# Four graph layers on one core: stages in another order, pieces of two PSUM banks, and a planner that keeps to a matmul form

## The chip, the core and the metric

One Trainium2 chip, one of its cores. The engines are TensorE (PE: matmuls and, beside them, its weight loads, PEld), VectorE (DVE), ScalarE (ACT), GpSimd (POOL) and SyncE (SP, which here only issues DMAs). The metric is device time of one execution in microseconds (us), the median of five runs.

## The reference, cut to what matters

x is 16 batches of 1024 nodes by 256 features; adj is one 1024 by 1024 adjacency matrix for all. Four layers follow each other, each of the form x = x + layer(relu(layernorm(x))):

```python
# layers 0, 1 (one head) and 3 (four heads): graph attention
h = x @ W;  e = leaky_relu((h @ a1)[:, None] + (h @ a2)[None, :])
x = x + act(softmax(where(adj, e, -big)) @ h)        # act: relu in layer 0, elu in 1 and 3
# layer 2: eight heads of 32
t = softmax(where(adj > 0, q @ k.T / sqrt(32), -big)) @ v
y = layernorm(h + t);  y = layernorm(y + relu(y @ w1 + b1) @ w2 + b2)
x = x + y
```

## The kernel before

A *stage* is one layer of one batch; there are 64. Work of a stage on TensorE:

- **Way in** (`way_in`, lines 700 to 760): for each of 8 tiles of 128 nodes, VectorE takes mean and variance (lines 663, 664), GpSimd the root (667, 668), ScalarE or VectorE normalises, TensorE transposes (`transpose_rows`, line 687, pieces of two tiles, copied out by ScalarE in line 690), and TensorE projects (`project`, line 697; pieces of one tile for graph attention, of half a batch for q and k).
- **Layers 0 and 1**, one head (`gat_item`): VectorE makes the unnormalised weights p (line 926), and TensorE multiplies them with the values (line 944, tile av, full 128 by 128 matmuls of 257 columns).
- **Layer 2**, the dot stage (`dot_item`): for a group of four heads and a tile of 128 nodes, TensorE makes scores of four heads in four row tiles of 32 rows (line 1147, tile sc), ScalarE takes the exp (1160), VectorE masks (1166), and TensorE sums values and totals into column tiles of 32 columns (lines 1178 and 1183). Then come a division (`dot_out`) and `feed_forward` with `finish`: two layernorms, w1 and w2.
- **Layer 3**, four heads in pairs (`pair_item`): weights on VectorE (line 1000), values (1032) and totals (1056) in column tiles of 32.

The source scores of graph attention are needed along a row by every partition. `sources` transposes them (line 873, tile tpr), VectorE copies them (877), SyncE writes them to DRAM (885 or 888) and reads them back spread over 128 partitions (899 or 904, tile r).

**The order is a planner's.** Every piece of work is an `op` with its engine, a cost, the ops it comes after, the buffers it takes and ends, and for TensorE a form: none (full), 132 (row tiles), 32 (column tiles). `forward` places ops one by one: on each engine it looks at the ops that can begin first, within SLACK, and takes the one of the lowest rank; a change of form is charged with SWITCH. `backward` turns the result into due times, which are the ranks of the next play. The best of PLAYS = 8 plays is what is emitted, so the planner's order is each engine's order on the chip.

Buffers are rings, of which a place is taken over from its last holder: p has 9 places of 1024 elements, y 2, hT 4, big 4. PSUM, eight banks, is split by use: sc two places of two banks (scores, and layer 3's totals), acc two of one bank, mm two of one bank (transposes and projections).

The stages were laid in this order:

```python
order = [(0, 0), (0, 1), (1, 0), (1, 1)]
for b in range(0, B, 2):
    order += [(2, b), (2, b + 1), (3, b), (0, b + 2), (3, b + 1), (0, b + 3), (1, b + 2), (1, b + 3)]
```

At the start, the first x, the adjacency (line 384) and layer 0's weights are loaded, VectorE turns the adjacency into flags (line 1372, twice, for != 0 and for > 0), TensorE transposes these (1378) and ScalarE copies them to the two masks (1382).

Of the kernel before, what the change touches and what calls it, by code (L numbers as in the profile page):

```python
# [285 lines left out]
def fast_path(tc, bad, x, adj, l0_w, l0_a, l1_w, l1_a, w_qkv, ln1_g, ln1_b, ln2_g, ln2_b, w1, b1, w2, b2, l3_w, l3_a, out):  # L286
# [3 lines left out]
    assert B % 2 == 0 and B > 2  # L290
# [9 lines left out]
    with ctx:  # L300
# [5 lines left out]
        ps_sc = ctx.enter_context(tc.tile_pool(name="ps_sc", bufs=2, space=PSUM))  # L306
        ps_acc = ctx.enter_context(tc.tile_pool(name="ps_acc", bufs=2, space=PSUM))
        ps_mm = ctx.enter_context(tc.tile_pool(name="ps_mm", bufs=2, space=PSUM))
# [38 lines left out]
        def gat_weights(group, w_heads, a, alpha, name):  # L347
# [10 lines left out]
            ab = work.tile([P, 2 * C], F32, tag="p", name="ab", bufs=9)  # L358
# [17 lines left out]
            return wx, [lambda h=h: fill(h) for h in range(heads)]  # L376

# [24 lines left out]
        b2_row = work.tile([P, 2 * C], F32, tag="p", name="b2_row", bufs=9)  # L402
# [12 lines left out]
        flags = state.tile([P, NT * C], F32, tag="y", name="flags").bitcast(BF16)  # L415
# [17 lines left out]
        SWITCH = {None: 0.15, 132: 0.2, 32: 0.12}  # L433
# [4 lines left out]
        SLACK = 0.2  # L438
# [5 lines left out]
        class Ring:  # L444
# [3 lines left out]
            def __init__(self, bufs, ordered=False):  # L448
                self.bufs, self.ordered, self.laid, self.first = bufs, ordered, 0, []

        class Hold:


            def __init__(self, ring, make, taken=False):
                self.ring, self.make, self.enders, self.taker, self.t = ring, make, [], None, None
                self.number, ring.laid = ring.laid, ring.laid + 1
                if taken:
                    ring.first.append(self)
                    self.t = make()
# [15 lines left out]
        def choose(open_ops, time, begin, key, slack):  # L475

            best = None
            for eng in range(5):
# [5 lines left out]
                if could:  # L484
                    last = min(c[0] for c in could) + slack
                    at, o = min((c for c in could if c[0] <= last), key=lambda c: key[c[1].number])
                    if best is None or at < best[0]:
                        best = (at, o)
# [4 lines left out]
        def forward(rank):  # L493
# [4 lines left out]
            taken = {ring: list(ring.first) for ring in R.values()}  # L498
# [6 lines left out]

            def begin(o):
# [3 lines left out]
                for i, h in enumerate(o.takes):  # L510
                    ring = h.ring
                    k = len(taken[ring]) + sum(g.ring is ring for g in o.takes[:i])
                    if ring.ordered and h.number != k:
                        return None
                    if k >= ring.bufs:
                        old = taken[ring][k - ring.bufs]
# [5 lines left out]
            for _ in ops:  # L522
                at, o = choose(open_ops, time, begin, rank, SLACK)
# [8 lines left out]
                for h in o.takes:  # L532
                    taken[h.ring].append(h)
                    left[h], free[h] = len(h.enders), 0.0
# [10 lines left out]
        def backward(total, played, taken):  # L545

            before = [list(o.after) for o in ops]
            for ring, holds in taken.items():
                for old, h in zip(holds, holds[ring.bufs :]):
                    before[h.taker.number] += [o for o in old.enders if o is not h.taker]  # L550
# [9 lines left out]
            for _ in ops:  # L560
                at, o = choose(open_ops, time, lambda o: ready[o.number], key, 0.0)
# [9 lines left out]
        def play():  # L571
            rank, best = [o.rank for o in ops], None
            for _ in range(PLAYS):
# [3 lines left out]
                rank = backward(*result)  # L577
            for _, _, o in best[1]:
                for h in o.takes:
                    h.t = h.make()  # L580
# [4 lines left out]
            "sc": Ring(2, True), "acc": Ring(2, True), "p": Ring(9, True), "r": Ring(2, True), "y": Ring(2, True),  # L585
            "big": Ring(4, True), "v0": Ring(1, True), "v1": Ring(1, True), "v2": Ring(1, True), "e": Ring(4),
            "mm": Ring(2), "xn": Ring(2), "hT": Ring(4), "stats": Ring(8), "rstd": Ring(8), "inv": Ring(4),
# [7 lines left out]
        def mm(name, shape=(P, HALF), dtype=F32):  # L595
            return psum(ps_mm, "mm", list(shape), name, dtype)

        def buffer(pool, tag, shape, name, dtype=F32):
            bufs = R[tag].bufs
            return Hold(R[tag], lambda: pool.tile(list(shape), dtype, tag=tag, name=name, bufs=bufs))  # L600

# [4 lines left out]
        class Stage:  # L606
# [9 lines left out]
            def buffers(self):  # L616
                L = self.layer

                pair, odd = divmod(self.b, 2)
                if pair == 0:  # L620
                    place = ((2, 1), (0, 2), (1, 0), (2, 1))[L][odd]
                else:
                    place = (3 - ((2, 2), (0, 1), (2, 0), (1, 2))[L][odd] - pair) % 3
                self.vh = buffer(state, f"v{place}", (P, NT * H2 * (D2 + 1)), "v")
                if L == 2:
                    self.qh = buffer(state, "big", (P, KC, N), "qT")
                    self.kh = buffer(state, "big", (P, KC, N), "kT")
# [5 lines left out]
                if L == 3:  # L633
                    self.rh = [buffer(state, "big", (P, 2, N), "r2") for _ in range(self.heads // 2)]
                if L in (2, 3):
                    self.yh = buffer(state, "y", (P, NT, C), "y")
# [19 lines left out]
        def stats_of(src, rank, after, shift=False):  # L656
# [15 lines left out]
            m_op = op(DVE, 0.54, rank, stats, after, takes=[mh, rh])  # L672
# [7 lines left out]
        def transpose_rows(srcs, rank, after, dst, t, func, scale=1.0, ends=()):  # L680

            tph = mm("tp", (P, KC, 2 * P))
# [6 lines left out]
            def copy():  # L689
                nc.scalar.activation(dst.t[:, :, t * P : (t + 2) * P], tph.t, func, scale=scale)  # L690

            a = op(PE, 0.44, rank, turn, after, takes=[tph], ends=ends)
            return op(ACT, 0.48, rank + 0.7, copy, [a], ends=[tph])
# [6 lines left out]
        def way_in(s, t, rank, after):  # L700
            L = s.layer
            n, i = t // TH, t % TH
            if t == 0:
                s.hTh, s.in_ops = {}, {}
                s.norms, s.turns, s.vals, s.vops, s.roots = {}, {}, {}, {}, {}
                s.lead, s.srcs = {}, {}
            if i == 0:
                s.hTh[n] = buffer(state, "hT", (P, KC, HALF), "hT")
            hT = s.hTh[n]
            xt = lambda: xs[s.b][:, t, :]  # L710
            m_op, r_op, mh, rh = stats_of(xt, rank, after, shift=L == 2)
# [3 lines left out]
            if L == 2:  # L715
# [5 lines left out]
                    [r_op] + before, takes=takes + ([s.yh] if t == 0 else []), ends=[mh, rh],  # L721
                )
            else:
                if t % 2 == 0:
                    s.xnh = buffer(work, "xn", (P, 2, C), "xn")
# [783 lines left out]
```

## Time and profile before

| | us |
|---|---|
| five runs, median (lowest to highest) | 4429.75 (4429.71 to 4431.37) |
| the profiled execution | 4429.66 |
| its span, first to last instruction | 4427.9 |
| TensorE busy | 4361.4 |
| VectorE busy | 3378.2 |
| ScalarE busy | 2075.2 |
| GpSimd busy | 1343.9 |

The profile is one execution. A page gives busy times, the chain of work that ended last, and groups of instructions. A timeline merges equal instructions that follow each other on an engine: start, length, engine, line, tiles, shapes, count, and in brackets how long the engine was idle before and who released it. A table of windows gives each engine's busy time in a stretch. Matmuls are pipelined and their ends are modelled, so a start is a better mark than an end. Each 32-bit matmul is two records, a transpose one. The granted TensorE clock was 0.996 on average.

### The profile page before, as it was taken

To read this page: it belongs to the slowest core of one execution; us is meant where nothing else is said; L and a number is where in the kernel's file an instruction comes from. 1 tells how busy PE (TensorE), PEld (TensorE's weight loads), DVE (VectorE), ACT (ScalarE), POOL (GpSimd) and SP (SyncE) were. 2 spreads that over 40 slices of the span, in tenths; PEclk is the share of its full clock that TensorE was granted. 3 is DMA by queue.
4 is the path that set the end of the run, shared out by engine and by line. 5 is a ranking of instruction groups with operands and counts; after the bars stand their busy time and mean duration, and the time that the engine had idled before them with its cause. 6 is when DMAs were issued, how large, how long until landed. Compare 5 with 4: busy or idle time off the path is not lost.

```text
span 4427.9 us, 71264 instructions
## 1 busy us (share of the span) xinstructions
PE 4361.4 (98%) x28090; PEld 2171.4 (49%) x28090; DVE 3378.2 (76%) x5835; ACT 2075.2 (47%) x3345; POOL 1343.9 (30%) x2025
## 2 busy tenths in 40 slices
PE   8999999999999999999999999999999999999998
PEld 6733467334673346633566335653356533565333
DVE  7568885788856887579875798757987579875898
ACT  4456334563345633456335563356533565335552
POOL 3223333233331333214332233312342123421341
PEclk9999999999999999999999999999999999999999
DMA  3000000000000001000110001000011000100001
GB/s 114 6 1 20 25 30 24 1 20 25 29 25 1 20 25 46 8 1 20 38 36 6 1 20 44 30 6 1 20 44 34 1 1 20 44 25 1 1 20 40
DMA packets 59910, 96.66 MB, mean 22 GB/s; under 512 B 6320, under 2 KB 41520, under 8 KB 59568
## 3 DMA queue, kind: packets, MB, share of 16 engines
q1 hardware_dynamic: 59152, 91.51, 6.1%
q8 instruction: 223, 3.65, 0.3%
q14 instruction: 119, 0.97, 0.1%
q10 hardware_dynamic: 416, 0.52, 0.0%
HBM read 74.84 MB, written 17.17 MB: 21 GB/s over the span
## 4 chain that ended last, share of the span: by engine, by line
PE 89%; DVE 7%; POOL 2%; issue 1%; ACT 1%; DMA 0%; DVEq 0%; SPq 0%; POOLq 0%; ACTq 0%
PE pm L697 21%; PE av L944 19%; PE sc L1147 11%; PE acc L1178 10%; PE sums L1183 9%; PE acc L1032 9%; PE sums L1056 4%; PE tp L687 3%; DVE pe L1166 2%; DVE p L1000 1%; POOL y L1242 1%; POOL rstd L668 1%; DVE y L678 1%; PE tpv L1098 1%; DVE st L663 1%
## 5 line engine op out<-in xcount | busy, mean ns | idle before, releaser
L1166 DVE TENSOR_TENSOR pe<-pe,mask_pos 128x1024 f32<-128x1024 f32 x1024 | 1223.5, 1234 | 343.5 <-ACT pe L1160 342.0
L1160 ACT ACTIVATE pe<-sc 128x1024 f32<-128x1024 f32 x1024 | 998.0, 1022 | 637.0 <-PE sc L1147 594.7
L944 PE MATMUL av<-v,p 128*128 128x257 f32 x4096 | 945.3, 380 | 0.2 <-DVE p L926 0.2
L944 PEld LDWEIGHTS av<-v,p 128*128 128x128 f32 x4096 | 763.4, 190 | 147.4 <-issue 40.9
L667 POOL TENSOR_SCALAR rstd<-stats 128x1 f32<-128x1 f32 x768 | 368.0, 479 | 1262.0 <-DVE stats L664 1238.4
L1000 DVE SCALAR_TENSOR_TENSOR p<-r,e,mask_pos 128x1024 f32<-128x1024 f32 x512 | 635.3, 1281 | 33.6 <-PE sums L1056 33.5
L1147 PE MATMUL sc<-qT,kT 32*128 32x512 f32 x4096 | 590.6, 640 | 0.0
L668 POOL TENSOR_TENSOR rstd<-rstd,minus_half 128x1 f32<-128x1 f32 x768 | 566.8, 738 | 64.0
L1178 PE MATMUL acc<-pe,v 128*32 128x512 f32 x4096 | 549.7, 604 | 0.0
L1183 PE MATMUL sums<-pe,pick 128*32 128x512 f32 x4096 | 538.4, 592 | 0.9 <-ACT o L966 0.9
L1032 PE MATMUL acc<-p,v 128*32 128x512 f32 x4096 | 465.2, 594 | 0.0
L697 PE MATMUL pm<-l_wx,hT 128*128 128x259 f32 (+1 forms) x1536 | 410.8, 398 | 6.0 <-ACT hT L690 2.9
L1242 POOL TENSOR_TENSOR y<-y,turned 128x512 f32<-128x512 f32 x64 | 106.2, 1680 | 1020.4 <-DVE turned L1235 1020.4
L697 PEld LDWEIGHTS pm<-l_wx,hT 128*128 128x128 f32 x1536 | 276.4, 190 | 193.9 <-issue 90.3
L1147 PEld LDWEIGHTS sc<-qT,kT 32*128 32x128 f32 x4096 | 166.6, 182 | 318.3 <-issue 150.3
L690 ACT ACTIVATE hT<-tp 128x512 f32<-128x512 f32 x320 | 190.6, 597 | 238.9 <-PE tp L687 238.5
L663 DVE BATCH_NORM_STATS2 st<-x 128x6 f32<-128x256 f32 x512 | 214.8, 420 | 95.2 <-POOL x L970 77.7
L1183 PEld LDWEIGHTS sums<-pe,pick 128*32 128x32 f32 x4096 | 135.7, 110 | 306.0 <-issue 298.5
L1032 PEld LDWEIGHTS acc<-p,v 128*32 128x32 f32 x4096 | 123.3, 110 | 275.5 <-issue 261.1
L697 PE MATMUL pm<-hT,qkv_sb 128*128 128x512 f32 x512 | 246.6, 606 | 0.0
L1056 PE MATMUL sums<-p,e 128*32 128x512 f32 x2048 | 246.4, 597 | 0.0
L970 POOL TENSOR_TENSOR x<-x,o 128x256 f32<-128x256 f32 x128 | 106.6, 833 | 423.5 <-ACT o L966 338.1
(101 smaller groups left out, 4099.5 us busy)
## 6 DMA issues: line engine op xcount, KB each, us to landing
r<-kept SPq DMA_DIRECT2D x64, 512.0 KB
x<-in_x_dram SPq DMA_DIRECT2D x32, 512.0 KB
r<-kept SPq DMA_DIRECT2D x64, 256.0 KB
out_dram<-x SPq DMA_DIRECT2D x64, 256.0 KB
edges<-in_adj_dram SPq DMA_DIRECT2D x8, 512.0 KB
kept<-rows_sb SPq DMA_DIRECT2D x128, 2.0 KB
qkv_sb<-in_L_gnn_w_qkv_dram SPq DMA_DIRECT2D x1, 768.0 KB
kept<-rows_sb SPq DMA_DIRECT2D x32, 4.0 KB
```

The source lines that it names most:

```text
L667: nc.gpsimd.tensor_scalar(rh.t, mh.t[:, 1:2], EPS, None, ALU.add)
L668: nc.gpsimd.tensor_tensor(rh.t, rh.t, minus_half, ALU.pow)
L697: nc.tensor.matmul(dst, lhsT=lhsT[:, k, :], rhs=rhs[:, k, :], start=(k == 0), stop=(k == KC - 1))
L944: nc.tensor.matmul(avh.t[:, : s.hs + 1], lhsT=phs[j // 2].t[:, j % 2, i * P : (i + 1) * P], rhs=s.v[:, j, h, :], start=(j == 0), stop=(j = ...
L1000: nc.vector.scalar_tensor_tensor(ph.t, s.rh[hp].t[:, hh, :], s.e[:, j, col : col + 1], mask_pos[:, j, :], ALU.max, ALU.mult)
L1032: nc.tensor.matmul(acc[n].t[(2 * hh + part) * W : (2 * hh + part + 1) * W, :], lhsT=s.v[:, jj, h, part * W : (part + 1) * W], rhs=p, start ...
L1056: both(lambda jj, n, hh, h, p: nc.tensor.matmul(sums.t[(2 * n + hh) * W : (2 * n + hh + 1) * W, 0, :], lhsT=s.e[:, jj, 2 * H + h : 2 * H + ...
L1147: nc.tensor.matmul(scs[pair].t[:, hh, :], lhsT=s.kh.t[r0 : r0 + D2, g, j * P : (j + 1) * P], rhs=s.qh.t[r0 : r0 + D2, g, cols], start=True ...
L1160: lambda pair=pair: nc.scalar.activation(phs[pair].t, scs[pair].t, AF.Exp, scale=SCALE2),
L1166: lambda pair=pair: nc.vector.tensor_tensor(phs[pair].t, phs[pair].t, mask(), ALU.mult), [ex], tiles=True,
L1178: nc.tensor.matmul(head(acc, i), lhsT=s.v[:, j, g * QUAD + i, :D2], rhs=p(i), start=(j == 0), stop=(j == NT - 1))
L1183: nc.tensor.matmul(head(sums, i), lhsT=pick[:, g, :], rhs=p(i), start=(g == 0 and j == 0), stop=(g == KC - 1 and j == NT - 1),)
```

## The change

- **Order of stages.** A dot stage is now followed by a stage of layer 1, then layer 3, then layer 0, so that one-head stages stand between the column-tiled ones:

```diff
-        for b in range(0, B, 2):
-            order += [(2, b), (2, b + 1), (3, b), (0, b + 2), (3, b + 1), (0, b + 3), (1, b + 2), (1, b + 3)]
+        order = [(0, 0), (0, 1), (1, 0), (1, 1), (2, 0), (0, 2), (3, 0)]
+        for b in range(1, B - 3):
+            order += [(2, b), (1, b + 1), (3, b), (0, b + 2)]
+        E = B - 1
+        order += [(2, E - 2), (1, E - 1), (0, E), (2, E - 1), (1, E), (3, E - 2), (2, E), (3, E - 1), (3, E)]
```

- **PSUM.** ps_sc and ps_mm go. Three places of two banks, u0 to u2, serve scores, totals, transposes and projections. A ring can now be a set, in which any free place is taken (also for y and hT):

```diff
-        ps_sc = ctx.enter_context(tc.tile_pool(name="ps_sc", bufs=2, space=PSUM))
-        ps_mm = ctx.enter_context(tc.tile_pool(name="ps_mm", bufs=2, space=PSUM))
+        ps_u = ctx.enter_context(tc.tile_pool(name="ps_u", bufs=1, space=PSUM))
...
-            "sc": Ring(2, True), "acc": Ring(2, True), "p": Ring(9, True), "r": Ring(2, True), "y": Ring(2, True),
+            "u": Ring(3, is_set=True), "acc": Ring(2, True), "p": Ring(4, True), "r": Ring(2, True), "y": Ring(2, is_set=True),
...
+        def banks(name):
+            return Hold(R["u"], lambda i: ps_u.tile([P, 2, HALF], F32, tag=f"u{i}", name=name))
```

- **Pieces of two banks.** Transposes of four tiles, not two; values of layer 2 for four tiles; q, k and the first feed-forward product for both blocks of 128 features; the second product for four tiles; graph-attention values for two tiles. Each is copied out by ScalarE in one instruction of 1024 elements where it was two of 512 (but not the feed-forward's relu). The p buffers become 4 places of 2048 elements.

```diff
-                for m in range(2 * KC):
-                    queries_keys(s, m, n, rank + 4.0 + 2.2 * m)
+                    two_values(s, n, rank + 2.3, turned)
+                    for m in range(2):
+                        queries_keys(s, m, n, rank + 4.0 + 4.2 * m)
...
-            scs = [psum(ps_sc, "sc", [P, 2, HALF], "sc") for _ in pairs]
-            phs = [buffer(work, "p", (P, 2, HALF), "pe") for _ in pairs]
+            scs = [banks("sc") for _ in pairs]
+            ph = buffer(work, "p", (P, QUAD, HALF), "pe")
```

- **The planner.** An op of another form than TensorE's last counts as due 4 us later than it is; the charges for a change of form and the slack are set anew:

```diff
-        SWITCH = {None: 0.15, 132: 0.2, 32: 0.12}
-        SLACK = 0.2
+        SWITCH = {None: 0.2, 132: 0.21, 32: 0.125}
+        SLACK = 0.1
+        STAY = 4.0
...
-                at, o = choose(open_ops, time, begin, rank, SLACK)
+                at, o = choose(open_ops, time, begin, lambda o: rank[o.number] + STAY * (o.eng == PE and o.form != form), SLACK)
```

- **Prologue.** For the first stage the row of source scores isn't sent through DRAM: TensorE multiplies the scores, broadcast to 128 columns, with the identity, and ScalarE copies the result. The small inputs and the flags use the two y buffers before these are needed:

```diff
+            if s is stages[0]:
+                s.rops = [spread_sources(s, n, rank, lead[n * TH : (n + 1) * TH]) for n in range(NH)]
+                return
...
+        def spread_sources(s, n, rank, lead):
+            pmh, held = psum(ps_acc, "acc", [P, HALF], "spread"), s.rh[n]
+            def product():
+                for i in range(TH):
+                    nc.tensor.matmul(
+                        pmh.t[:, i * P : (i + 1) * P], lhsT=s.e[:, n * TH + i, 0:1].to_broadcast([P, P]), rhs=ident,
+                        start=True, stop=True,
+                    )
+            a = op(PE, 1.0, rank, product, lead, takes=[pmh], ends=[s.eh])
+            return op(ACT, 0.48, rank + 1.0, lambda: nc.scalar.copy(held.t, pmh.t), [a], takes=[held], ends=[pmh])
```

## The prediction

> **What bounds the kernel now.** I read the page first, then TensorE's timeline, the table of windows, and the ends of the run.
>
> ```profile
> PE 4361.4 (98%) x28090; PEld 2171.4 (49%) x28090; DVE 3378.2 (76%) x5835; ACT 2075.2 (47%) x3345; POOL 1343.9 (30%) x2025
> ...
> PE 89%; DVE 7%; POOL 2%; issue 1%; ACT 1%; DMA 0%; DVEq 0%; SPq 0%; POOLq 0%; ACTq 0%
> ```
>
> TensorE is busy for 98% of the span and is 89% of the chain that ended last. VectorE, at 76%, is second. So the time moves by what TensorE spends, or waits, and by little else. How TensorE spends it is seen in 14 us of its timeline (start, length, line, tile, matmuls):
>
> ```profile
> 1475.22 1.14 PE L1147 MATMUL sc<-qT,kT 32*128 32x512 f32 x8
> 1476.29 1.07 PE L1178 MATMUL acc<-pe,v 128*32 128x512 f32 x8
> 1477.17 1.04 PE L1183 MATMUL sums<-pe,pick 128*32 128x512 f32 x8
> 1478.03 1.04 PE L1178 MATMUL acc<-pe,v 128*32 128x512 f32 x8
> 1478.89 1.04 PE L1183 MATMUL sums<-pe,pick 128*32 128x512 f32 x8
> 1479.86 1.14 PE L1147 MATMUL sc<-qT,kT 32*128 32x512 f32 x8
> 1480.93 1.06 PE L1178 MATMUL acc<-pe,v 128*32 128x512 f32 x8
> 1481.81 1.04 PE L1183 MATMUL sums<-pe,pick 128*32 128x512 f32 x8
> 1482.78 1.99 PE L697 MATMUL pm<-w_sb,hT 128*128 128x256 f32 x8
> 1484.71 1.14 PE L1147 MATMUL sc<-qT,kT 32*128 32x512 f32 x8
> 1485.78 0.66 PE L687 MATMUL tp<-ident,xn 128*128 128x128 f32 x4
> 1486.37 1.06 PE L1178 MATMUL acc<-pe,v 128*32 128x512 f32 x8
> ```
>
> The lengths are modelled, so the distance from start to start is the cost. There are three forms: full (128 rows by 128 columns), row-tiled (32 by 128, the scores) and column-tiled (128 by 32). Column-tiled followed by column-tiled costs 0.86 (1477.17 to 1478.03), followed by another form 0.97 (1478.89 to 1479.86): **leaving it costs 0.11**. Scores cost 1.07 before either form, so leaving them costs nothing that is seen. Eight full matmuls of 256 columns cost 1.93 (1482.78 to 1484.71). Sixteen of 257 cost 3.68:
>
> ```profile
> 1302.39 3.74 PE L944 MATMUL av<-v,p 128*128 128x257 f32 x16
> 1306.07 1.14 PE L1147 MATMUL sc<-qT,kT 32*128 32x512 f32 x8
> ```
>
> The difference of 1.75 for eight gives 0.219 each, so 1.93 holds 0.18 that doesn't grow with the work. The same from 512 columns (four 1.92, eight 3.63) gives 0.21, and from transposes (four 0.59, eight 1.02) 0.16. **A visit to the full form costs about 0.195 with matmuls first, 0.16 with transposes first.**
>
> **The change, part by part.** *Form changes.* In the two programs' instruction order I counted unbroken stretches of one form. Stretches of the full form fall from 680 to 256 (matmuls first 398 to 135, transposes first 282 to 121), because projections now come in two-bank pieces, one-head stages stand between dot stages instead of pairs of dot stages side by side, and the planner keeps to a form. Column-tiled stretches fall from 677 to 547. The matmuls are the same but for eight of 128 columns. Saved: 263 x 0.195 = 51.3, 161 x 0.16 = 25.8, 130 x 0.11 = 14.3, together 91.4. The lowest readings (0.18, 0.16, 0.10) give 86, the highest (0.21, 0.18, 0.114) 99. I take **-93 us**.
>
> The Trainium skill (TensorEngine Tiling (Array Packing), Key Properties) says that changing the tiling mode, not just the tile, drains TensorE, which would price every change alike. All stretches together fall from 1869 to 1299, and 570 x 0.11 would be 63, for 4340. The trace disagrees in that leaving the scores costs nothing, and a visit to the full form more.
>
> *Prologue.* Before, layer 0's first weights wait for VectorE to make all 16 mask flags:
>
> ```profile
> 35.84 5.39 DVE L926 SCALAR_TENSOR_TENSOR p<-r,e,mask_nz 128x512 f32<-128x512 f32 x8
> ...
> 37.16 0.65 PE L944 MATMUL av<-v,p 128*128 128x257 f32 x2
> ```
>
> In the new order eight of the flags (1.14 us apart) come behind these weights, and the row is spread by TensorE and copied by ScalarE, not sent through DRAM (26.30 to beyond 29.39 before). The adjacency has landed by 18 us, so the data allow it. VectorE's work from 9.5 us to the first weights is 14 us: six fills 2.1, three stats 1.8, eight flags 9.1, six small ones 1.3. The first weights then begin near 23.5 and the first av, four weights later, near 27, 10 us earlier. But VectorE remains the fullest engine over the first 60 us of TensorE's work, so part is paid back. I take **-8** (-11 to -3). If the flags still came first it would be 0.
>
> *Stalls.* For each of TensorE's records I took the distance to the next over the lower quartile for the same pair of neighbours. Those over 0.1 us sum to 92 us between 45 and 4412: 40 in the first 1090 us, 17 in the last 550, and 6 to 8 in each 545 us between. The windows agree:
>
> ```profile
> 590.00:1140.00 550.00, 541.16 (x3474) 269.97 (x3466) 416.91 (x710) 255.82 (x413) 171.97 (x249) 0.99 0.06 20
> 1140.00:1685.00 545.00, 542.47 (x3498) 268.85 (x3494) 417.18 (x714) 257.55 (x416) 168.99 (x252) 1.00 0.06 20
> ...
> 4300.00:4428.00 128.00, 110.49 (x895) 40.75 (x891) 111.70 (x164) 24.67 (x45) 18.76 (x30) 0.94 0.11 35
> ```
>
> The first count is TensorE, the third VectorE. Nothing moves off VectorE. I cut both programs into slices of 60 us of undisturbed TensorE work and gave each VectorE instruction its row's mean (these overlap: they sum to 3656 where 3378 are busy). The fullest slice of the middle asks for 1.13 of TensorE's time before and 1.08 after, 1.04 and 1.00 after the overlap: dot (heavy) now alternates with one-head (light). What gets tighter is layer 3's row. Its way before, in the last stage, where nothing else hides it:
>
> ```profile
> 4352.40 0.28 PE L873 MATMUL tpr<-ident,e 128*96 128x128 f32 x1 [0.53 <-DVE v L825]
> ...
> 4354.27 2.95 SPq L888 DMA_DIRECT2D kept<-rows_sb  x8
> 4358.26 1.76 SPq L904 DMA_DIRECT2D r<-kept  x4
> ...
> 4370.71 3.64 PE L1032 MATMUL acc<-p,v 128*32 128x512 f32 x32
> ```
>
> Undisturbed it is: transpose and copy 0.8 (tpr at 2055.8, SP at 2056.57), stores 2.65, 1.1 until the loads issue, 4 until the first half lands (packets until 4362 to 4363), four weights 4.9: 13.5 to 14. The new order puts 11.4 us of TensorE work between this transpose and layer 3's first matmuls; before, it was 41 or more except in the last stage. Behind those stand layer 3's sums, so TensorE waits: 2.5 us in each of 13 repeats, 33. Stalls at the start and the transitional last batches I put at 15, the tail at 25 (17 before), since the last 100 us now ask VectorE for 1.10 of TensorE's time where before it was 1.02. Together 73 for 92: **-19**. From nearly all gone (25) to 157 (8 a repeat, the late chain below) the term is -67 to +65.
>
> *At nothing:* larger evacuations. ScalarE's 512-wide copies (0.597) become 256 of 1024 (1.02 by the exp's row), cheaper per element, at 47% busy; queued dot or av pieces cover the longer hold. The coarser p buffers (4 of 2048 in place of 9 of 1024) are paid in the stalls' range.
>
> A rule speaks against this. The Trainium skill (Perfetto Trace Analysis, Optimizing Scalar/DVE Operations) says that where ScalarE or VectorE isn't saturated but causes bubbles elsewhere, breaking instructions up may let work be completed sooner; the change joins them. If TensorE waited the added 0.42 for each of the 256, it would be 108 and the time 4418.
>
> **Sum.** The profiled execution took 4429.66 (span 4427.9 and 1.8 around it), against the median of 4429.75, so no correction. 4429.7 - 93 - 8 - 19 = **4310**.
>
> **Rivals.** *The forecast*, 4285 to 4345: 60%.
>
> *The row and its chain come late.* In the last stage before, it is 70.5 us from the last dot sums (4300.2) to layer 3's first matmul; the new order has 65 us of TensorE work there. If that pace holds everywhere, 5.5 us more are lost in each of 13 repeats: +72, 4382 (4345 to 4420). For it: the pieces are coarser, so four tiles wait for the slowest. Against: that chain shared VectorE with a full layer-3 stage. 17%.
>
> *Stalls nearly vanish*, as light stages cover the feed-forward chain that costs most now (tp waiting for y): 73 falls to 25, 4262 (4250 to 4285). 16%.
>
> *Slower, by the shared places.* Scores own four banks now; then they, projections and transposes share three places of two. Waits for places exist already where no full-form piece stands between:
>
> ```profile
> 1458.41 1.37 PE L1147 MATMUL sc<-qT,kT 32*128 32x512 f32 x8
> ```
>
> Its 1.37 against 1.14 is 0.23 of waiting for the second exp. Were that paid by all 512 score pieces, it would be 118 and the time 4428; above 0.25 each the change loses, and at 0.4 it gives 4515. Against: with a third place free the next scores need only the first exp, which ends 1 us before they are due, and the third is held only around some 8 projections and transposes per dot stage. 5%, with 2% more for ending within 0.2%.
>
> *Forms not kept* is excluded by the counted order.
>
> Faster by over 0.2% (about 9 us, what a measurement here can tell from no change) is 0.93, the same 0.02, slower 0.05. The range runs from the third case's 4262 to 4380, through the second's own value nearly; what it leaves out is half of the third case, nearly half of the second, and the last.
>
> **What would show it.** After: 1.07 per score piece and about 0.88 and 0.97 for column pieces, unchanged; about 256 stretches of the full form; the first av near 27 us; TensorE's busy time down by about 90; a gap of 2 to 3 us before layer 3's first matmul in each 262-us repeat, released by VectorE's weights. Wrong if score pieces stretch to 1.37 throughout, if the gap per repeat is 8 us or more, or if VectorE ends the chain for long stretches.

## The result and the profile after

| | before | after |
|---|---|---|
| median (lowest to highest), us | 4429.71 (4428.44 to 4431.7) | 4420.42 (4419.07 to 4422.61) |
| runs | 44 | 24 |
| span of the profiled execution | 4427.9 | 4418.7 |
| granted clock, mean | 0.996 | 0.988 |

The ratio is 0.9979 (95% interval 0.9974 to 0.9985): 9.3 us faster, where 120 were forecast. The page of the changed kernel, engines and chain of waits:

```profile
PE 4316.0 (98%) x28105; PEld 2230.8 (50%) x28105; DVE 3377.7 (76%) x5834; ACT 2002.8 (45%) x3091; POOL 1274.2 (29%) x2025
...
PE 92%; DVE 5%; ACT 2%; POOL 1%; issue 1%; DMA 0%; DVEq 0%; SPq 0%; ACTq 0%; POOLq 0%
```

TensorE's busy time fell by 45 us, not by the 90 forecast, and it still ends nearly everything. The lines don't tell whether its work shrank less than thought or whether waits took the place of work. Two views do. The table of windows (TensorE, its weight loads, VectorE, ScalarE, GpSimd, then the granted clock):

```profile
590.00:1140.00 550.00, 540.08 (x3517) 281.00 (x3516) 422.37 (x728) 252.51 (x392) 165.27 (x265) 0.99 0.06 20
1140.00:1685.00 545.00, 534.44 (x3468) 274.58 (x3467) 415.47 (x703) 245.21 (x378) 158.14 (x243) 0.99 0.06 20
4290.00:4418.00 128.00, 108.95 (x879) 41.38 (x871) 109.94 (x160) 22.68 (x40) 19.60 (x30) 0.92 0.10 34
```

TensorE now stands visibly in the middle of the kernel: 10.6 us of the 545 between 1140 and 1685, where it had stood 2.5. The waits by releaser (engine, line and tile that waited, who released it: us, times, longest):

```profile
PE tp L719 <- ACT y L752: 43.0, 24, 2.3
PE pm L726 <- ACT hT L722: 19.9, 17, 2.1
PE tp L719 <- ACT xn L772: 8.5, 2, 7.3
PE count L1550 <- DVE broken L1548: 6.8, 1, 6.8
PE sc L1211 <- ACT pe L1225: 5.9, 19, 0.6
PE tp L719 <- DVE y L710: 5.7, 9, 1.1
PE acc L1091 <- DVE p L1057: 2.4, 2, 1.6
```

The wait that the prediction added, layer 3's matmuls for VectorE's weights, is the last line: 2.4 us in the whole run. The largest is one it hadn't priced: the dot stage's transposes wait for ScalarE's y, 43 us.

**Work and waits apart.** For each kernel I took TensorE's instruction order and gave each instruction the undisturbed distance (lower quartile) that the kernel before has for the same pair of neighbours. That sum is called *work* here, and *waits* is what the time from first to last matmul has over it.

| | work | waits | first to last matmul |
|---|---|---|---|
| before | 4293.4 | 121.4 | 4414.8 |
| after | 4195.9 | 209.3 | 4405.2 |
| difference | -97.5 | +87.9 | -9.6 |

In the first 45 us the waits fell from 15.6 to 6.3; from 45 to 545 they stayed (19.6, 20.0); from 545 to 3932 they rose from 61.7 to 146.9, and from there to the end from 24.5 to 36.0. So the saving is there, and it is given back in the middle: 10 to 14 us in each repeat of some 273 us (of which some 262 are work) from 800 on, where before had about 4 in as long a stretch.

**One repeat.** TensorE's timeline of the changed kernel where layer 1's last products, the dot stage's way in and layer 3 meet:

```profile
2520.24 0.27 PE L915 MATMUL tpr<-ident,e 128*96 128x128 f32 x1
2520.35 3.65 PE L1001 MATMUL av<-v,p 128*128 128x257 f32 x16
2523.83 0.60 PE L719 MATMUL tp<-ident,y 128*128 128x128 f32 x4
2525.67 0.44 PE L719 MATMUL tp<-ident,y 128*128 128x128 f32 x2 [1.24 <-ACT y L752]
2528.45 0.69 PE L719 MATMUL tp<-ident,y 128*128 128x128 f32 x2 [2.34 <-ACT y L752]
2530.25 5.71 PE L726 MATMUL pm<-qkv_sb,hT 128*128 128x256 f32 x16 [1.11 <-ACT hT L722]
2535.80 3.60 PE L726 MATMUL pm<-hT,qkv_sb 128*128 128x512 f32 x8
2539.33 3.64 PE L1091 MATMUL acc<-p,v 128*32 128x512 f32 x32
```

The four tiles are one piece. The last av ends near 2524.0 and only then can the last tile's y begin: reciprocal 2524.03, exp and relu 2524.29 and 2524.67, two adds to 2525.76, statistics to 2526.44, GpSimd's root to 2527.77, y 2527.80 to 2528.40. Nothing else is queued on TensorE between the av and these transposes, so it stands for this chain and for the copy behind it: 5.5 us over the undisturbed distances. Then the projection that takes 3.5 from start to start elsewhere takes 5.6. The windows just before and after say why:

```profile
2520.30:2527.00 6.70, 4.57 (x24) 3.60 (x22) 3.67 (x13) 2.17 (x5) 1.46 (x5) 1.00 0.12 40
2527.00:2533.80 6.80, 4.23 (x10) 3.14 (x11) 4.56 (x4) 1.62 (x2) 0.66 (x2) 0.54 0.74 272
```

The granted clock (third number from the end) is 1.00 in the first and 0.54 in the second. The clock record has such half-clock windows, of 3.41 or 6.83 us, from 600 to 3650 us once in each repeat, right behind this place. Without the last one, at the end of the run, there are 16, 92 us in all, against 5 and 27 before.

Layer 3 has its first weights at 2529.24 (released by the row's DMA) and four of them at 2534.3, 14 us after tpr as forecast. But its matmuls begin 19.1 us after tpr. The row isn't what TensorE waits for; the y chain came first.

### The profile page after: what moved, and what is told of

Same layout as the page of the kernel before. It is cut to its first block, busy times and chain, and to the rows that moved or that the text cites. A ratio compares the mean times of both kernels' runs of the same rounds, so it can differ in the third digit from the quotient of the medians.

```text
span 4418.7 us, 70358 instructions
## 1 busy us (share of the span) xinstructions
PE 4316.0 (98%) x28105; PEld 2230.8 (50%) x28105; DVE 3377.7 (76%) x5834; ACT 2002.8 (45%) x3091; POOL 1274.2 (29%) x2025
## 4 chain that ended last, share of the span: by engine, by line
PE 92%; DVE 5%; ACT 2%; POOL 1%; issue 1%; DMA 0%; DVEq 0%; SPq 0%; ACTq 0%; POOLq 0%
PE pm L726 21%; PE av L1001 20%; PE sc L1211 12%; PE acc L1245 11%; PE acc L1091 10%; PE sums L1250 9%; PE sums L1115 5%; PE tp L719 3%; DVE pe L1233 2%; PE tpv L1154 1%; PE tpo L1276 1%; DVE st L695 1%; ACT pe L1225 0%; DVE y L710 0%; ACT hT L722 0%
## 5 line engine op out<-in xcount | busy, mean ns | idle before, releaser
L1057 DVE SCALAR_TENSOR_TENSOR p<-r,e,mask_pos 128x1024 f32<-128x1024 f32 x512 | 623.8, 1279 | 134.0 <-PE sums L1115 104.8
L699 POOL TENSOR_SCALAR rstd<-stats 128x1 f32<-128x1 f32 x768 | 324.0, 422 | 1256.9 <-DVE stats L696 1233.4
L1211 PE MATMUL sc<-qT,kT 32*128 32x512 f32 x4096 | 600.9, 639 | 6.0 <-ACT pe L1225 5.9
L1245 PE MATMUL acc<-pe,v 128*32 128x512 f32 x4096 | 563.5, 604 | 0.3
L1250 PE MATMUL sums<-pe,pick 128*32 128x512 f32 x4096 | 550.9, 592 | 0.0
L726 PE MATMUL pm<-l_wx,hT 128*128 128x259 f32 (+1 forms) x1536 | 373.0, 391 | 5.5 <-ACT hT L722 5.4
L1310 POOL TENSOR_TENSOR y<-y,turned 128x512 f32<-128x512 f32 x64 | 90.4, 1433 | 925.7 <-DVE turned L1303 925.7
L726 PEld LDWEIGHTS pm<-l_wx,hT 128*128 128x128 f32 x1536 | 287.4, 191 | 97.0 <-issue 33.3
L1245 PEld LDWEIGHTS acc<-pe,v 128*32 128x32 f32 x4096 | 88.7, 108 | 345.0 <-DVE pe L1233 151.9
L772 ACT ACTIVATE xn<-x,stats 128x256 f32<-128x256 f32 x256 | 127.6, 508 | 270.5 <-DVE stats L696 249.2
```

Source lines behind the costliest of these rows:

```text
L699: nc.gpsimd.tensor_scalar(rh.t, mh.t[:, 1:2], EPS, None, ALU.add)
L726: nc.tensor.matmul(dst, lhsT=lhsT[:, k, :], rhs=rhs[:, k, :], start=(k == 0), stop=(k == KC - 1))
L1057: nc.vector.scalar_tensor_tensor(ph.t[:, hh, :], s.rh[hp].t[:, hh, :], s.e[:, j, col : col + 1], mask_pos[:, j, :], ALU.max, ALU.mult)
L1211: nc.tensor.matmul(scs[pair].t[:, hh, :], lhsT=s.kh.t[r0 : r0 + D2, g, j * P : (j + 1) * P], rhs=s.qh.t[r0 : r0 + D2, g, cols], start=True ...
L1245: nc.tensor.matmul(head(acc, i), lhsT=s.v[:, j, g * QUAD + i, :D2], rhs=p(i), start=(j == 0), stop=(j == NT - 1))
L1250: nc.tensor.matmul(head(sums, i), lhsT=pick[:, g, :], rhs=p(i), start=(g == 0 and j == 0), stop=(g == KC - 1 and j == NT - 1),)
```

## The theories

- **A**: the new order of stages puts the dot stage's transposes right behind the av pieces whose results they need, so TensorE stands for y's chain. The trace has this wait of 1.24 and 2.34 us in twelve repeats.
- **B**: layer 3's row would hold TensorE there anyway, so without the y chain the wait moves.
- **C**: the shared PSUM places cost, where scores wait for exps.
- **D**: the half clock follows from the standing and has a price of its own.
- Rivals that came up later, **E** to **I**, on the pieces, the planner and the PSUM places, are stated in the expectations of the runs that test them.

## Experiments

All times are medians; "before" was run beside each on the same chip (4428.9 to 4430.4). e1, e2, e3 and e5 keep the changed kernel's order of instructions on TensorE, and e11 keeps e8's but for a few matmuls at the end; in the others the planner planned anew.

### e1: y without its normalisation

```diff
-  lambda: nc.scalar.activation(src(), xt(), AF.Relu, scale=rh.t, bias=mh.t[:, 1:2]),
+  lambda: nc.scalar.activation(src(), xt(), AF.Relu),
```

> The changed kernel in its own instruction order, but the dot stages' way-in is y = relu(x): the first normalisation of layer 2 is left out of y (its statistics and root are still computed, and y no longer waits for them). Theory A (TensorE stands in its queue at the dot stage's transposes until the last y, and a half-clock window follows): the last y needs only the second add, which ends near 2525.8 in the repeat measured, so it is there near 2526.4 in place of 2528.4: 2.0 us for each of 15 repeats, 30, and if the shorter stall brings no half-clock window (2.2 us) another 33: 4357 to 4390. Theory B (layer 3's row through DRAM would hold TensorE there anyway): the time stays at 4420, and the wait moves to layer 3's first matmul. Theory C (scores waiting for shared PSUM places): 4420, nothing moves.

Measured: 4392.21, ratio to before 0.9915 (0.99 to 0.9931), 28.2 less than the changed kernel. Its timeline at the same place:

```profile
2501.23 0.60 PE L719 MATMUL tp<-ident,y 128*128 128x128 f32 x4
2502.89 0.44 PE L719 MATMUL tp<-ident,y 128*128 128x128 f32 x2 [1.06 <-ACT y L752]
2503.66 0.44 PE L719 MATMUL tp<-ident,y 128*128 128x128 f32 x2 [0.33 <-DVE st L695]
2505.21 6.64 PE L726 MATMUL pm<-qkv_sb,hT 128*128 128x256 f32 x16 [1.11 <-ACT hT L722]
```

The wait of 2.34 is 0.33, 2.0 us in each of twelve repeats. All but 4 of the 31 us by which the time from first to last matmul fell lie in line 719. A holds for the shorter wait (30 forecast, 28 came; 4392 is 2 us above its range). The half-clock windows got shorter, 65 us in 13 where there were 92 in 16, but most stayed, so that part of its range didn't come. C as the main cause, which expected no move, falls.

### e2 and e3: layer 3's row early

```diff
             def store():
-                kept.append(dram.tile([H3, NT, P], F32, tag="kept", name="kept"))
+                if s.layer == 3:
+                    if s.b > 0:
+                        kept.append(row3[0])
+                        return
+                    row3.append(dram.tile([H3, NT, P], F32, tag="kept3", name="kept3", bufs=1))
+                    kept.append(row3[0])
+                else:
+                    kept.append(dram.tile([H3, NT, P], F32, tag="kept", name="kept"))
```

> The changed kernel in its own order, but layer 3's stages from the second on store no row and load the first one's, which has long been in DRAM: it leaves out their own source rows. Theory B: the 2.5 us forecast for each of 13 repeats go, 4387. Theory A: the row was no longer what came last (its first weights begin at 2529.2 and four are done at 2534.3, layer 3's first matmul is at 2539.3), so 4420 within 5. Theory C: 4420.

> Both edits of the two runs before it together. Theory A: with y early, TensorE would reach layer 3 some 4 us sooner, at about 2535, still after the row's weights (2534.3): the same as with y alone, within 10, so 4350 to 4390. Theory B, in the form that y and the row hold TensorE one behind the other: y alone gives nothing, both together 33 to 60: 4360 to 4387. Theory C: 4420.

Measured: e2 (normal y) 4465.41, ratio 1.0082 (1.0066 to 1.0097), **45 us more** than the changed kernel. e3 (row early and plain y) 4386.51, ratio 0.9898 (0.9882 to 0.9913); its runs spread from 4380.94 to 4390.31, and the traced one, the slowest, has e1's time from first to last matmul (4374.6 in both). B falls as it stands: with y's chain whole, taking away the row's wait gains nothing, and with the chain shortened at most the 5.7 us between the medians of e1 and e3. e1 still has layer 3's matmuls 15 to 18 us behind tpr, later than the row's 14, so these two runs don't tell what the row would cost if y's whole stall were gone. That an early row costs was in no theory. GpSimd in e2, where the last tile's root is made:

```profile
1160.95 1.17 POOL L699 TENSOR_SCALAR rstd<-stats 128x1 f32<-128x1 f32 x1 [2.35 <-DVE stats L696]
1162.20 1.46 POOL L700 TENSOR_TENSOR rstd<-rstd,minus_half 128x1 f32<-128x1 f32 x1
1163.76 1.91 POOL L702 TENSOR_SCALAR stats<-stats,rstd 128x1 f32<-128x1 f32 x1
```

and TensorE behind it:

```profile
1160.10 0.44 PE L719 MATMUL tp<-ident,y 128*128 128x128 f32 x2 [1.24 <-ACT y L752]
1166.36 0.69 PE L719 MATMUL tp<-ident,y 128*128 128x128 f32 x2 [5.82 <-ACT y L752]
```

The same three instructions take 0.22, 0.57 and 0.27 in the changed kernel. In e2 VectorE, not held by the row any more, goes from the last statistics at 1160.68 straight into layer 3's weights (eight of 1.2 us from 1160.78), and GpSimd's root, between 1160.95 and 1165.67, takes 4.7 us where it took 1.3. The wait grows by 3.48 in each of twelve repeats, 42 of the 43 us by which the time from first to last matmul grew. The Trainium skill (GPSIMD Engine Reference, Specifications) says that GpSimd shares its SBUF interface with VectorE and contends with VectorE instructions of two SBUF inputs; these weights read r and the mask, and the row agrees. So in the changed kernel the row's lateness, which I had priced as a loss, kept VectorE out of the root's way. And e2 shows once more that y's chain is what TensorE waits for. In e3, where y needs no root, the early row is harmless.

### e5: TensorE kept busy while it waits

```diff
                 for u, src in enumerate(srcs):
+                    for k in [0, 1] * fill[u]:
+                        nc.tensor.transpose(tph.t[:, k, u * P : (u + 1) * P], srcs[0]()[:, k * P : (k + 1) * P], ident)
```

with fill (0, 0, 5, 10) for the second four tiles of a dot stage, and zeros elsewhere.

> The changed kernel in its own order, with 30 more transposes in each dot stage's way-in: 10 ahead of the third tile's and 20 ahead of the fourth tile's, of a tile of y that is there already, into places that the real ones overwrite. They fill the two waits of 1.24 and 2.34 us (0.109 each by the trace: 1.1 and 2.2 us). Theory D (the granted clock halves for 3.4 or 6.8 us because TensorE stood for several us just before, which costs 2.2 us in a repeat): with TensorE busy the window goes, 12 or 13 repeats give -26 to -29, about 4393. If the window doesn't follow the standing, or the filler delays what it covers: 4420 to 4430. If the filler didn't fit into the waits at all it would cost 52: 4472.

Measured: 4406.11, ratio 0.9946 (0.9931 to 0.9961): 480 useless transposes made the kernel 14.3 us faster. The windows of e5 at the same place in the repeat:

```profile
2511.00:2518.00 7.00, 6.85 (x47) 6.12 (x46) 3.51 (x11) 2.17 (x5) 1.85 (x5) 1.00 0.15 47
2518.00:2524.80 6.80, 5.53 (x28) 4.31 (x27) 4.87 (x5) 2.14 (x3) 0.27 (x1) 1.00 0.71 264
```

The clock is 1.00 in both. From 400 us to 3680 e5 gains 1.4 to 2.7 us in each of twelve repeats, 25.6 together, and the y chain still ends when it did; the filler costs 5.1 in the first batches and 7.3 in the last ones, where there was less to fill. In these repeats D holds, at about the size forecast (26 to 29), and the half clock is a second price on the same stall; the whole kernel gained 14.3, less by what the filler costs elsewhere, which the forecast of 4393 left out.

### e4 and e8: another stage in between

```diff
-        order = [(0, 0), (0, 1), (1, 0), (1, 1), (2, 0), (0, 2), (3, 0)]
-        for b in range(1, B - 3):
-            order += [(2, b), (1, b + 1), (3, b), (0, b + 2)]
+        order = [(0, 0), (0, 1), (1, 0)]
+        for b in range(B - 3):
+            order += [(2, b), (1, b + 1), (0, b + 2), (3, b)]
...
+        PLACES = {key: key[1] % 3 for key in by_key}
```

This is e8; e4 has the same groups to the end (each b with those of its four stages that exist) where e8 keeps the changed kernel's last nine stages.

> The changed kernel with another order of stages: layer 0's one-head stage of batch b+2 goes ahead of layer 3 of batch b, so that some 27 us of TensorE work that needs neither can stand between layer 1's last av pieces and the dot stage's transposes, and between layer 3's row and its first matmul. The computation is the reference's. Theory A: most of the 5.5 us of standing and 2.2 us of half clock in each of some 13 repeats goes, 100 at most; the hiccup of about 2.4 us per repeat behind the scores stays: 4330 to 4375. Theory B: 33 go, 4387. Theory C: places are shared as before, 4420.

> The order that was faster (layer 0's stage ahead of layer 3), with the changed kernel's own order of the last nine stages in place of that one's: there it had lost some 65 us to waits after 3932, where the changed kernel lost 36. The computation is the reference's. Theory A: the middle keeps 4 us of waiting in each repeat, the tail loses 30 less: 4330 within 12. If the tail's waits come with the middle's order instead: 4359.

Measured: e4 4359.29, ratio 0.984 (0.9827 to 0.9854). **e8 4321.86, ratio to before 0.9755 (0.9742 to 0.9768)**: 107.9 us faster than before and 98.6 faster than the changed kernel. e4's own last stages cost it the 37.4 between the two. TensorE of e8 at the place in question:

```profile
2745.05 0.27 PE L915 MATMUL tpr<-ident,e 128*96 128x128 f32 x1
2745.16 3.62 PE L726 MATMUL pm<-qkv_sb,hT 128*128 128x256 f32 x16
2748.61 3.64 PE L1001 MATMUL av<-v,p 128*128 128x257 f32 x16
2752.09 1.03 PE L719 MATMUL tp<-ident,y 128*128 128x128 f32 x8
2752.96 1.91 PE L1001 MATMUL av<-v,p 128*128 128x257 f32 x8
2754.70 3.61 PE L726 MATMUL pm<-qkv_sb,hT 128*128 128x256 f32 x16
```

Two av pieces of layer 0 (3.64) now stand in front of the four transposes, which come whole and without a bracket: the y chain runs beneath them. Over their copy, ahead of the projection, stands one more (1.91). tpr is 43.6 us ahead of layer 3's first matmul (18 to 19.6 in most repeats of the changed kernel). The waits of e8, its three longest kinds:

```profile
PE sc L1211 <- ACT pe L1225: 9.2, 24, 0.5
PE tp L719 <- ACT xn L772: 8.0, 3, 7.4
PE count L1547 <- DVE broken L1545: 6.8, 1, 6.8
```

The line of 43 us is gone (0.2 remain). Work is 4194.0 and waits 113.1, against 4293.4 and 121.4 before; before the tail, the clock record has no half-clock window at all. With waits 8 us below before's, about what the prologue gained, the time falls by the work saved and little more: this is the forecast's largest term, seen as time.

### e11: e8 with plain y

e1's diff on e8.

> The kernel with the fastest order, with y = relu(x) in the dot stages' way-in: the first normalisation of layer 2 is left out of y. Theory A: in this order other work stands ahead of the dot stage's transposes, so y's chain ends in time and a shorter one gives nothing: 4322 within 4 (in the changed kernel's order the same edit gave 28). If the chain still held TensorE: 4295 to 4310.

Measured: 4320.85, ratio 0.9756 (0.974 to 0.9772): 1.0 from e8, where the same edit gave 28 in the changed order. The y chain is off the path.

### e6, e7, e9: one part alone, or one part less

e6 is the kernel before with the changed order (the diff of the front), its places and what it needs; e9 is before with the planner's diff alone; e7 is the changed kernel with `STAY = 0.0`.

> The kernel before with the changed kernel's order of stages alone (and what that order needs: its v places, the later allocation of the large buffers, y held from its statistics on, more buffers for statistics). Pieces of one PSUM bank, transposes of two tiles, the old planner and the old prologue stay. From the rows of the kernel before, TensorE's work without waits is 4262 in its order (before 4293, the changed kernel 4196); 15 us lie around it, and the waits were 121 before and 209 after. Theory A in the form that the order of stages makes the waits: 4262 + 209 + 15 = 4486, less up to 30 because two-tile transposes need two tiles of y only: 4455 to 4490, slower than before. Rival E, that the four-tile pieces make them: 4262 + 121 + 15 = 4398.

> The changed kernel with the planner's price for leaving a matmul form, STAY, at 0 in place of 4. Its order has 336 stretches of the full form (256 with 4) and 612 column stretches (547); without waits TensorE's work is 4216 by the rows of before, 20.5 more. Theory A (the waits come from the order of stages, not from keeping to a form): 4420 + 20 = 4441 within 10. Rival F (keeping to a form starves the other engines and so makes the waits): the waits fall by more than 20 and the time is below 4420, 4355 at the least if they go back to 121.

> The kernel before with the planner's part of the change alone (STAY 4, the new prices for a change of form, SLACK 0.1). Its order of stages, pieces and prologue stay. TensorE's stretches of the full form fall from 680 to 616 only, and its work without waits from 4293 to 4280.5 by the rows of before. If keeping to a form makes no waits of its own: 4430 - 13 = 4417 within 6. If it starves the others (rival F): 4430 or more.

| | us | ratio to before (95%) | work | waits |
|---|---|---|---|---|
| e6, order alone | 4521.64 | 1.0208 (1.0192 to 1.0223) | 4262.1 | 242.6 |
| e9, planner alone | 4493.52 | 1.0146 (1.0129 to 1.0163) | 4280.5 | 198.1 |
| e7, changed, STAY 0 | 4449.31 | 1.0043 (1.0028 to 1.0059) | 4216.4 | 220.2 |

e6 was slower than A's range, and E's 4398 is far off: the order alone makes waits, with small pieces too. But they aren't A's. Two lines of e6's waits:

```profile
PE tp L685 <- DVE y L676: 35.4, 44, 1.5
...
PE tp L685 <- ACT y L721: 1.3, 2, 1.0
```

The second is the y of the dot stage's way in, 43 us in the changed kernel (42.9 in e7); the first is the feed-forward's y, 13.5 before. With two-tile transposes and the old planner the same order has projections between the last av and the last transposes, where the changed kernel has nothing. So y's stall needs the order together with some of the other parts. The four-tile pieces, which wait for the slowest of four, are the likely one, as E had it; they weren't tried by themselves. e7 loses 29 to the changed kernel, 20.5 of it work as forecast and 11 more waits: keeping to a form makes no waits there (F falls). But e9, which I expected to gain 13, lost 64: on the old kernel the planner's new rules do make waits, as F said, though e9 changes SWITCH and SLACK with STAY and doesn't tell them apart. Of its 77 us of new waits 69 lie at the dot stages' own lines (scores 39.8, values 38.1, totals 23.1, where before had 8.9, 17.5, 5.7).

### e10, e12, e13: pieces and places

e10 is before with e8's order alone, e12 is e10 with the changed planner, and e13 is e8 with two shared places:

```diff
-            "u": Ring(3, is_set=True), "acc": Ring(2, True), ...
+            "u": Ring(2, is_set=True), "acc": Ring(2, True), ...
```

> The kernel before with the order of stages that was fastest (4321.9), and what the order needs, alone: pieces of one bank, two-tile transposes, old planner, old prologue. Its stretches of the full form are 321 (that kernel: 216), TensorE's work without waits 4211 (that kernel: 4194). Theory A (waits come from the order of stages): waits like that kernel's 113, so 4211 + 113 + 15 = 4339, up to 10 more for the old prologue: 4335 to 4355. Rival G (in an order of single stages the small pieces make waits of their own, as the order alone had 243): 4469.

> The kernel before with the fastest order of stages and also the changed planner (STAY 4, new prices, SLACK 0.1); only the pieces, the PSUM places (two for scores, two of one bank for the rest) and the prologue are still the old ones. TensorE's work without waits is 4213 by the rows of before. Theory H (the waits of 312 us come from the old pieces and places: with two places for scores the next score piece waits for the last exp, 0.63 us for each two pieces in a bare dot stretch): still 4500 to 4550. Rival I (they come from the old planner's rules): the waits fall to some 120, 4350.

> The fastest kernel with two shared PSUM places of two banks in place of three (two banks stand empty); pieces, planner and the order of the stages are the same, the order of the instructions is planned anew. TensorE's work without waits is 4206 by the rows of before (4194 with three). Theory H (the third place is what lets scores run ahead): at least 0.63 us for each of 256 pairs of score pieces, 161, and more where projections take one of the two: 4495 to 4700. If places are not what limits: 4322 + 12 = 4334.

| | us | ratio to before (95%) | work | waits | of these at dot lines |
|---|---|---|---|---|---|
| e10 | 4536.61 | 1.0238 (1.0221 to 1.0255) | 4211.3 | 311.8 | 205 |
| e12 | 4612.55 | 1.0411 (1.0394 to 1.0428) | 4212.9 | 381.8 | 229 |
| e13 | 4749.83 | 1.0721 (1.0704 to 1.0739) | 4206.3 | 528.5 | 441 |
| e8 | 4321.86 | 0.9755 (0.9742 to 0.9768) | 4194.0 | 113.1 | 71 |

A's expectation of e10 (4335 to 4355) was far off. G and H were right in direction and too small: 4469 expected of e10, 4500 to 4550 of e12, at most 4700 of e13. The best order on the old pieces, with 82 us less work than before, is 107 us slower than before. TensorE of e10 in a dot stage:

```profile
2744.85 1.37 PE L1148 MATMUL sc<-qT,kT 32*128 32x512 f32 x8
2746.15 1.47 PE L1179 MATMUL acc<-pe,v 128*32 128x512 f32 x8
2747.03 1.45 PE L1184 MATMUL sums<-pe,pick 128*32 128x512 f32 x8
2748.41 1.14 PE L1148 MATMUL sc<-qT,kT 32*128 32x512 f32 x8
2749.48 1.06 PE L1179 MATMUL acc<-pe,v 128*32 128x512 f32 x8
2750.37 1.04 PE L1184 MATMUL sums<-pe,pick 128*32 128x512 f32 x8
2751.34 1.37 PE L1148 MATMUL sc<-qT,kT 32*128 32x512 f32 x8
```

Every second round is stretched: 6.49 us for two, against 5.86 undisturbed. A score piece is two tiles of two banks, and the old kernel has two such places, so the next one waits for the exps of the last (1.37) and what follows waits for the mask (1.47, 1.45). Before, full-form pieces stood between and covered it; an order with fewer changes of form takes this cover away. In e8 the same bare rounds run unstretched:

```profile
2594.04 1.14 PE L1211 MATMUL sc<-qT,kT 32*128 32x512 f32 x8
2595.11 1.06 PE L1245 MATMUL acc<-pe,v 128*32 128x512 f32 x8
2595.99 1.04 PE L1250 MATMUL sums<-pe,pick 128*32 128x512 f32 x8
2596.96 1.14 PE L1211 MATMUL sc<-qT,kT 32*128 32x512 f32 x8
```

because the third place lets half the next score piece go ahead. Take it away (e13) and the scores wait for each exp, in TensorE's timeline:

```profile
2615.32 1.14 PE L1211 MATMUL sc<-qT,kT 32*128 32x512 f32 x8
2617.57 2.04 PE L1211 MATMUL sc<-qT,kT 32*128 32x512 f32 x8 [1.11 <-ACT pe L1225]
2619.83 2.99 PE L1211 MATMUL sc<-qT,kT 32*128 32x512 f32 x8 [0.21 <-ACT pe L1225]
```

e13 loses 428 us to e8, but it has one place fewer for transposes and projections as well, so that isn't the price of the scores' place alone. Half clock is in it too: the clock records of e12 and e13 have 160 and 164 us of it, where before had 27. e12 tells that the old planner's rules aren't the cause of e10's waits (rival I falls): with the new ones they are larger.

## Why the prediction was wrong

Its signs and its mechanism of gain were right, its sum wrong by one term: **the stalls**.

- **Form changes, -93: right.** Work fell by 97.5 by the rows. As time it is seen only in e8, where waits are near those of before: -99.4 of work in -107.9 of time. e7 gives the planner's share: 20.5 of work for STAY. The drain rule of the Trainium skill (TensorEngine Tiling (Array Packing), Key Properties), priced there at the trace's 0.11 a change, would have given 63; with the stretches of e8 (216 of the full form, 563 column-tiled, 1278 in all) it would give 591 x 0.11 = 65, and e8's work fell by 99.
- **Prologue, -8: right.** The first av is at 27.44 (near 27 forecast), and the waits of the first 45 us fell by 9.3.
- **Stalls, 92 to 73: the step that failed.** By the same measure (distances over 0.1 us, 45 to 4412) they are 198, +106 where -19 was forecast and +65 was the upper bound. The step took the 11.4 us of TensorE work between tpr and layer 3's matmuls as a block without gaps and asked only whether the row would be later. Inside that block stand the dot stage's transposes, which need the av pieces just ahead of them. The row's own time, 13.5 to 14 us, was right, and no one waits for it. In place of 2.5 us in each of 13 repeats for the row there are 5.5 for y's chain and 2.2 for the half clock that follows, in each of twelve: some 92 together. The remaining hiccup of some 2.4 at the start of the feed-forward, where score pieces stand side by side, is there in the trace; it wasn't tried alone. The start was put at 15 with the transitional last batches, and the last 100 us at 25; 20 between 45 and 545 and 24 after 4193 fit.
- **Why it was missed.** Before's own waits showed where to look: tp waiting for y led its list, 13.5 us of feed-forward. The prediction named it, and took it for a thing that light stages would cover. The changed order was on paper: for each piece the question was how far ahead on TensorE's queue its last producer stands. For the row that was asked; for y it wasn't. It is the av piece right ahead, with nothing behind it but two tiles' transposes, for a chain of 4.4 us and a copy of 1.0. And the pieces had just been made to wait for four tiles at once: with two-tile pieces in the same order (e6) this wait is 1.3 us in the whole run.
- **The rivals.** "The row and its chain come late" had nearly the right size, 5.5 more per repeat, and the wrong chain, counted from the dot stage's last sums; its upper end, 4420, is the result by luck. Its argument, that four tiles wait for the slowest, is what the transposes do. "Slower, by the shared places" (whose break-even is 120/512, 0.23 us a score piece, not 0.25) read a true row (1.37 for 1.14) and turned it the wrong way: two places of their own made that wait, and the third shared one removes it (e10, e13 against e8). It doesn't follow that sharing is free: the changed kernel's dot lines still wait 62 us (32 before).
- **At nothing: the larger evacuations.** They wait at the transposes' copy for 19.9 us where it was 10.7, mostly behind y's stall; in e8 it is 5.0. The estimate from the Trainium skill's advice to break instructions up (Perfetto Trace Analysis, Optimizing Scalar/DVE Operations) gave 4418, next to the result, by a mechanism that the runs don't show: e8 keeps every joined copy and takes 4322.
- **The signs listed.** Score pieces of 1.07 and 256 stretches held. TensorE's busy time fell by 45, since waits inside a merged piece and matmuls at half clock count as busy. The gap per repeat was set at 8 us or more as proof of error; it is 7.7 with the half clock, before layer 3, but released by y.

That the parts need each other also stood in no step. Order alone +92, planner alone +64, the best order on old pieces +107, all parts -9, all parts with the best order -108: too few places for running ahead cost little until the order takes the cover away, and an order that saves form changes is worth nothing until the places are there.

What stays open: which part beside the order makes y's stall, why e6 and e12 wait as much as they do outside the dot lines, and whether the hiccup at the feed-forward can be had too.

## What to carry to other kernels

When an order is changed so that an engine switches less, list for each piece in the new order the last producer it needs and count the engine's work between them: a piece that comes within the length of its producer's chain is a stall, and here the first such stall, y's, hid the next, the row's. Price a stall of several us on TensorE with the half clock that follows. A cover that is removed shows up in another place's shortage, so parts of a change aren't additive and one part's loss alone says little on the whole.

## What the runs showed of the hardware

- **The clock halves behind short gaps.** In the changed kernel windows of 3.41 and 6.83 us at half clock followed a place where TensorE stood 1.24, 2.34 and 1.11 us with matmuls between; no single gap was longer than 2.34. Filling the first two with useless transposes took away all twelve windows from 600 to 3650 us. In e2, with a gap of 5.82, most windows were 10.2 us. The Trainium skill (TensorE: Matmul & The Clock Gate, What's actually happening) gives a free-running window of 3413 ns; the lengths agree with one, two and three of it.
- **VectorE's large instructions stretch GpSimd's smallest.** One-element-per-partition instructions of GpSimd went from 0.22, 0.57 and 0.27 us to 1.17, 1.46 and 1.91 beside VectorE's 128x1024 weights (e2), and 42 us of the run hung on it.
